# Scores and value products of a windowed attention kept together in TensorE's queue, with a new order of stages

## The chip, the cores and the metric

The kernel runs on one core of a Trainium2 chip. The metric is the device time of one execution, in microseconds (us). TensorE (PE in the profile, its weight loads PEld) multiplies matrices, VectorE (DVE), ScalarE (ACT) and GpSimd (POOL) do the work on elements, and SyncE (SP) issues nearly all transfers. Each engine takes its own queue strictly from the front.

## The reference

Eight sequences of 1024 tokens with 256 features, float32, pass through two blocks, each followed by a residual sum and a layer norm:

```
x = layernorm(x + attn(x))            # one causal head of width 64, biases, 8 x 1024 x 256
x = layernorm(x + ffn(x))             # ffn: two layers of:
    h   = shift_token(x)              # second half of the features comes from the token before
    q, k, v = split(h @ wqkv)         # 8 heads of 64
    q, k = l2norm(q)*qs, l2norm(k)*ks, then rotated and scaled by position
    o   = softmax over a window: a tile of 128 tokens sees itself and the tile before it
    x   = x + o @ wo
    h   = layernorm(shift_token(x)) * lg + lb
    a, g = split(h @ w1 + b1);  x = x + (a * gelu(g)) @ w2 + b2        # 682 hidden features
```

## The kernel before, in words

Matrix products of float32 precision are made of three products in a faster format: each operand is split into a high part (ScalarE, `halves`, L92) and a low part (VectorE, L93), and `products` (L104 does the matmuls) adds high x high, high x low and low x high in PSUM.

The program has two parts. `fronts` does the first attention and takes about the first 260 us; the change does not reorder it. `layers` does the two windowed layers. It walks over 128 tiles of 128 tokens (2 layers x 8 sequences x 8 tiles), two tiles in one pass of a loop, 64 pairs in all. A pass does not finish one pair: it runs a list of stages, `ORDER`, in which each entry names a stage and how far ahead of the current tile w it works. `("sc", -2, 0)` is the first half of the scores of tile w-2, `("qk", 1, 0)` the first half of the q and k of tile w+1. The stages:

- `prep` (L677): transposes two tiles of x (`l_xp`) into `l_xT`.
- `qk` (two halves, `l_pqk`): six matmuls of 512 columns; then ScalarE squares (L705), VectorE sums the squares (`l_ss`, L708) and multiplies twice by the rotary table (`l_t`, L715), GpSimd adds (L722).
- `v` (`l_pv`): six matmuls; ScalarE copies.
- `unit`: the inverse norms, a chain of ten small VectorE operations (`l_nrm_*`, L112 to L129), and two GpSimd products (L733).
- `turn` (two halves, `l_t`, L756): four transposes of q and k, split into `ring`.
- `sc` (two halves u, four heads each, `l_sc`, L785): twelve matmuls, whose operands have 64 rows. Heads go in pairs: one uses the upper, one the lower 64 rows of the array. Then, for each head, VectorE applies mask and scale in place and takes the extreme value (`l_nm`, L793), and ScalarE takes the exponential into `l_e` (L654). After the second half the inverse of the sums goes through DRAM and comes back spread over the partitions as `l_R` (L805 to L816).
- `et` (two halves, `l_et`, L832): eight transposes of e, copied by ScalarE into `l_eT` (L835).
- `val` (two halves, `l_po`, L849): eight matmuls of e and v, whose outputs have 64 partitions. Each is recorded as two passes.
- `out`: `l_po` times `l_R` on VectorE (`l_on`, L858), split on ScalarE (L863) and GpSimd (L864).
- `proj` (`l_py`): twelve matmuls, and VectorE adds x (L879).
- `side`: one step of the feed-forward of an earlier pair: norm and transposes (`m_hp`, L931), six steps of the first product (`m_pag`, L104; gelu on ScalarE, L966 and L969 on VectorE, L970 on GpSimd), two steps of the second product (`m_pf`, 17 matmuls each) and the end (L988). In the second layer the final norm (`o_*`) follows.

PSUM has eight banks. Four are the buffers of `l_sc` (`PSB["sc"]`); one half of a tile's scores takes two of them. The other four (`ps`) are shared by everything else that TensorE writes.

`ORDER` gives priorities, not the queues themselves. A planner that knows the data dependencies and models durations sets each engine's queue, and moves instructions of one stage between those of another where it expects an engine to be free. No order among matmuls is asked for beyond the data dependencies.

Of the kernel before, what the change touches and what calls it, by code (L numbers as in the profile page):

```python
# [28 lines left out]
def kernel(  # L29
# [31 lines left out]
    nc = tc.nc  # L61
# [33 lines left out]
    def products(dst, pairs):  # L95
# [4 lines left out]
        passes(dst, steps)  # L100

    def passes(dst, steps):
        for i, (a, b) in enumerate(steps):
            nc.tensor.matmul(dst, a, b, start=(i == 0), stop=(i == len(steps) - 1))  # L104

# [388 lines left out]
    def load_ffn(l, stage, ps, W):  # L494
# [22 lines left out]
        for c in range(2):  # L517
            pb = ps(f"pb1_{l}_{c}")
            for k in range(2):
                for m0, m1 in ((0, NF - 1), (NF - 1, NF + 1)):  # L520
# [4 lines left out]
                    for m in range(m0, m1):  # L525
                        z = P if m < NF else LEFT
                        q = 0 if m < NF else k * OFF
                        u = (m - m0) * P
                        nc.tensor.matmul(
                            pb[q : q + z, k * 8 + m : k * 8 + m + 1],  # L530
                            st[:, u : u + z], lgb[:, 1, c : c + 1], start=True, stop=True,
                        )
# [54 lines left out]
    ORDER = [  # L587
        ("side", 1), ("out", -4), ("side", 1), ("side", 1), ("unit", -1), ("proj", -4),
        ("unit", -2), ("turn", -2, 0), ("turn", -1, 0), ("turn", -1, 1), ("sc", -2, 0),
        ("turn", -2, 1), ("qk", 0, 0), ("out", -3), ("side", 1), ("sc", -2, 1), ("side", 1),  # L590
        ("side", 1), ("proj", -3), ("sc", -1, 0), ("qk", 0, 1), ("v", 1), ("et", -2, 0),
        ("sc", -1, 1), ("et", -2, 1), ("v", 0), ("et", -1, 0), ("val", -2, 0), ("et", -1, 1),
        ("prep", 2), ("qk", 1, 0), ("side", 1), ("side", 1), ("qk", 1, 1), ("val", -1, 0),
        ("val", -2, 1), ("val", -1, 1), ("side", 1), ("side", 1), ("side", 1),
    ]

    def layers(pool, psum):
# [59 lines left out]
        def attention(l, b, W, finished):  # L657
# [4 lines left out]
            def prep(p):  # L662
# [12 lines left out]
                for c in range(2):  # L675
                    for j in range(2):
                        nc.tensor.transpose(  # L677
                            pt[:, c, j * P : (j + 1) * P], xl[:, j, c * P : (c + 1) * P], ident
                        )
# [66 lines left out]
            def turn(t, k):  # L746
# [7 lines left out]
                for c in range(4):  # L754
                    cols = slice(c * P, (c + 1) * P)
                    nc.tensor.transpose(pt[:, cols], r[:, cols], ident)  # L756
                hi, lo = [x[:, :, 2 * k : 2 * k + 2, slot, :] for x in ring]
                halves(hi, lo, pt.rearrange("p (s c q) -> p s c q", s=2, c=2))

            def scores(w, u):  # L760
# [19 lines left out]
                for j in range(2):  # L780
                    c = 2 * u + j
                    for m, (x, y) in enumerate(((0, 0), (0, 1), (1, 0))):
                        for i in range(2):
                            rows = slice(i * DH, (i + 1) * DH)
                            nc.tensor.matmul(  # L785
                                sc[i][:, j, 0:nk], ring[x][rows, 0, c, slot, :],
                                ring[y][rows, 1, c, keys, :], start=(m == 0), stop=(m == 2),
                            )
                for j in range(2):
# [33 lines left out]
            def turn_e(w, u):  # L823
# [4 lines left out]
                for j in range(2):  # L828
                    pt = ps(f"{n}_et{j}").rearrange("p (a i q) -> p a i q", a=2, q=P)
                    for a in range(m):  # L830
                        for i in range(2):
                            nc.tensor.transpose(  # L832
                                pt[:, a, i, :], e[:, i, j, a * P : (a + 1) * P], ident
# [4 lines left out]
            def values(w, u):  # L838
# [5 lines left out]
                for j in range(2):  # L844
                    c = 2 * u + j
                    for a, t in enumerate(order):
                        for i in range(2):
                            head = 2 * c + i
                            nc.tensor.matmul(  # L849
                                po[i * DH : (i + 1) * DH, c * P : (c + 1) * P],  # L850
                                st["v", t][:, head * DH : (head + 1) * DH], eT[:, j, a, i, :],
                                start=(a == 0), stop=(a == len(order) - 1),
                            )

# [34 lines left out]
        def feed_forward(l, b, p, x1, W):  # L889
# [39 lines left out]
            for c in range(2):  # L929
                for j in range(2):  # L930
                    nc.tensor.transpose(  # L931
                        pt[:, c, j * P : (j + 1) * P], hn[:, j, c * P : (c + 1) * P], ident
# [100 lines left out]

        PAIRS = DEPTH * B * NT // 2

        run("prep", 0)
# [76 lines left out]
```

## Time and profile before

| | |
|---|---|
| median of 3 runs | 2795.12 us (2794.61 to 2795.77) |
| the profiled execution | 2790.89 us, span 2789.1 us, mean granted clock 0.984 |
| TensorE matmuls | busy 2703.2 us (97%), 22336 records |
| TensorE weight loads | busy 2350.4 us (84%) |
| VectorE | busy 2440.2 us (87%) |
| ScalarE | busy 1748.8 us (63%) |
| GpSimd | busy 1245.9 us (45%) |
| first transpose of `layers`, first one of the last pair | 261.5 us, 2661.9 us |

Busy is the time in which at least one instruction of the engine runs. Matmuls are pipelined: a matmul lasts 0.28 us in the records, but the next one starts 0.11 to 0.12 us after it. So the durations of matmuls don't add up to time, and the distance from one start to the next (the pitch) is what counts. "Idle before" is the time before an instruction in which its engine did nothing, with the releaser that ended it.

### The profile page before, as it was taken

To read this page: it belongs to the slowest core of one execution; us is meant where nothing else is said; L and a number is where in the kernel's file an instruction comes from. 1 tells how busy PE (TensorE), PEld (TensorE's weight loads), DVE (VectorE), ACT (ScalarE), POOL (GpSimd) and SP (SyncE) were. 2 spreads that over 40 slices of the span, in tenths; PEclk is the share of its full clock that TensorE was granted. 3 is DMA by queue.
4 is the path that set the end of the run, shared out by engine and by line. 5 is a ranking of instruction groups with operands and counts; after the bars stand their busy time and mean duration, and the time that the engine had idled before them with its cause. 6 is when DMAs were issued, how large, how long until landed. Compare 5 with 4: busy or idle time off the path is not lost.

```text
span 2789.1 us, 63147 instructions
## 1 busy us (share of the span) xinstructions
PE 2703.2 (97%) x22336; PEld 2350.4 (84%) x22336; DVE 2440.2 (87%) x8464; ACT 1748.8 (63%) x4486; POOL 1245.9 (45%) x1515
## 2 busy tenths in 40 slices
PE   7998999999999999999999999999999999999997
PEld 5776688888888888888888788888888888888886
DVE  6887789888889988889888899999999999999995
ACT  6675566666666666666666566666666666666663
POOL 4553244444444444344453444444444454444442
PEclk9999899999999999999999999999999999999998
DMA  6332011011111111111111111111111111111110
GB/s 181 97 98 86 26 39 43 28 43 43 43 41 39 34 38 43 43 41 39 37 57 52 57 51 49 39 41 49 51 50 40 39 48 50 51 41 43 43 47 24
DMA packets 146126, 139.83 MB, mean 50 GB/s; under 512 B 28680, under 2 KB 122768, under 8 KB 145808
## 3 DMA queue, kind: packets, MB, share of 16 engines
q1 hardware_dynamic: 144448, 135.32, 16.0%
q8 instruction: 176, 2.88, 0.4%
q14 instruction: 142, 1.16, 0.1%
q10 hardware_dynamic: 1360, 0.46, 0.1%
HBM read 95.35 MB, written 27.81 MB: 44 GB/s over the span
## 4 chain that ended last, share of the span: by engine, by line
PE 69%; DVE 22%; ACT 3%; DMA 3%; issue 2%; POOL 0%; SPq 0%; DVEq 0%; POOLq 0%; ACTq 0%
PE l_pqk L104 11%; PE m_pag L104 9%; PE m_pf L104 9%; PE l_sc L785 8%; PE l_et L832 7%; PE l_po L849 6%; PE l_pv L104 5%; PE l_py L104 4%; PE l_t L756 3%; DVE l_t L715 3%; DVE m_gl L966 3%; DVE m_a L969 2%; DVE l_nrm_p L127 1%; DVE l_ss L708 1%; DVE l_sc L793 1%
## 5 line engine op out<-in xcount | busy, mean ns | idle before, releaser
L722 POOL TENSOR_TENSOR l_t<-l_t,l_t 128x256 f32<-128x256 f32 x512 | 367.5, 739 | 855.1 <-DVE l_t L715 816.0
L654 ACT ACTIVATE l_e<-l_sc,l_nm 128x256 f32<-128x256 f32 (+1 forms) x992 | 450.6, 462 | 288.4 <-DVE l_nm L793 279.3
L104 PE MATMUL m_pag<-m_hT,w_h 128*128 128x256 f32 (+1 forms) x2816 | 515.1, 285 | 6.4 <-DVE l_t L715 3.3
L793 DVE CUSTOM_DVE_ANT_0 l_sc<-l_sc,mask,l_nrm_y 128x256 f32<-128x256 f32 (+1 forms) x1024 | 453.6, 470 | 50.6 <-ACT l_e L654 36.0
L104 PEld LDWEIGHTS m_pag<-m_hT,w_h 128*128 128x128 f32 (+1 forms) x2816 | 430.3, 187 | 21.1 <-issue 10.5
L654 ACT ACTIVATE m_gl<-m_pag,b 128x256 f32<-128x256 f32 (+1 forms) x384 | 181.4, 474 | 385.2 <-PE m_pag L104 332.6
L104 PE MATMUL m_pag<-m_hT,w_l 128*128 128x256 f32 (+1 forms) x1408 | 393.7, 280 | 0.0
L104 PE MATMUL l_pqk<-wqk_h,l_xT 128*128 128x512 f32 x1024 | 392.4, 424 | 0.8 <-ACT l_xT L92 0.8
L715 DVE TENSOR_TENSOR l_t<-l_pqk,l_tab 128x512 f32<-128x512 f32 x512 | 329.8, 680 | 0.0
L835 ACT COPY l_eT<-l_et 128x512 f32<-128x512 f32 (+1 forms) x512 | 276.0, 567 | 80.6 <-PE l_et L832 56.3
L970 POOL TENSOR_TENSOR m_a<-m_gl,m_a 128x256 fp32r<-128x256 f32 x320 | 241.4, 762 | 113.2 <-DVE l_nrm_h L125 55.4
L832 PE MATMUL l_et<-ident,l_e 128*128 128x128 f32 x1920 | 269.9, 279 | 4.4 <-ACT l_eT L835 3.4
L104 PEld LDWEIGHTS m_pag<-m_hT,w_l 128*128 128x128 f32 (+1 forms) x1408 | 264.7, 188 | 0.0
L832 PEld LDWEIGHTS l_et<-ident,l_e 128*128 128x128 f32 x1920 | 215.2, 141 | 49.9 <-ACT l_eT L835 13.3
L104 PE MATMUL m_pf<-w_h,m_a 128*128 128x256 f32 x1280 | 249.5, 284 | 0.0
L849 PE MATMUL l_po<-l_eT,l_v 128*64 128x128 f32 x3840 | 242.0, 278 | 0.7 <-ACT l_eT L835 0.6
L104 PEld LDWEIGHTS l_pqk<-wqk_h,l_xT 128*128 128x128 f32 x1024 | 196.0, 191 | 53.9 <-ACT l_xT L92 1.2
L849 PEld LDWEIGHTS l_po<-l_eT,l_v 128*64 128x64 f32 x3840 | 209.5, 138 | 35.2 <-issue 18.8
L104 PEld LDWEIGHTS m_pf<-w_h,m_a 128*128 128x128 f32 x1280 | 203.5, 188 | 11.0 <-POOL m_a L970 0.2
L864 POOL TENSOR_TENSOR l_oT<-l_on,l_oT 128x512 fp32r<-128x512 f32 x128 | 165.0, 1289 | 97.5 <-ACT l_oT L863 92.6
L785 PE MATMUL l_sc<-ring,ring 64*128 64x256 f32 (+1 forms) x2048 | 207.5, 283 | 0.0
L104 PE MATMUL l_py<-wo_h,l_oT 128*128 128x256 f32 x1024 | 205.0, 282 | 0.0
(195 smaller groups left out, 6636.4 us busy)
## 6 DMA issues: line engine op xcount, KB each, us to landing
l_R<-rd_d SPq DMA_DIRECT2D x256, 128.0 KB
x<-x_d SPq DMA_DIRECT2D x96, 256.0 KB
l_tab<-tab_d SPq DMA_DIRECT2D x128, 128.0 KB
xin<-in_L_attn_x_dram SPq DMA_DIRECT2D x16, 512.0 KB
x_d<-xin SPq DMA_DIRECT2D x16, 512.0 KB
rd_d<-l_rT SPq DMA_DIRECT2D x512, 1.0 KB
x_d<-x SPq DMA_DIRECT2D x32, 256.0 KB
out_dram<-x SPq DMA_DIRECT2D x32, 256.0 KB
```

The source lines that it names most:

```text
L104: nc.tensor.matmul(dst, a, b, start=(i == 0), stop=(i == len(steps) - 1))
L654: ins = nc.scalar.activation(*args, **kw)
L715: nc.vector.tensor_tensor(tt[j].rearrange("p (k h d) -> p k h d", k=2, d=DH), p3, tb.unsqueeze(2).to_broadcast([P, 2, HEADS // 2, DH]), AL ...
L722: nc.gpsimd.tensor_add(a[:, :, s, :], a[:, :, s, :], bsw[:, :, 1 - s, :])
L756: nc.tensor.transpose(pt[:, cols], r[:, cols], ident)
L785: nc.tensor.matmul(sc[i][:, j, 0:nk], ring[x][rows, 0, c, slot, :], ring[y][rows, 1, c, keys, :], start=(m == 0), stop=(m == 2),)
L793: nc.vector.tensor_tensor_reduce(dst, dst, mk, st["nrm", w][:, 8 * u + h : 8 * u + h + 1], BIG, ALU.add, ALU.min, nm[:, one],)
L832: nc.tensor.transpose(pt[:, a, i, :], e[:, i, j, a * P : (a + 1) * P], ident)
L835: nc.scalar.copy(eT[:, j, 0:m], pt[:, 0:m])
L849: nc.tensor.matmul(po[i * DH : (i + 1) * DH, c * P : (c + 1) * P], st["v", t][:, head * DH : (head + 1) * DH], eT[:, j, a, i, :], start=(a ...
L864: nc.gpsimd.tensor_tensor(oT[1], on, oT[0].bitcast(FP), ALU.subtract)
L970: nc.gpsimd.tensor_tensor(a[1], gl[0:z, :], a[0].bitcast(FP), ALU.subtract)
```

## The change

Two things change, both in `layers`; all arithmetic and all instructions that compute stay.

First, the matmuls and transposes of TensorE go through small wrappers, which add order edges from the start of `layers` on. An edge of this kind is no wait on a semaphore; it only tells the planner which of two TensorE instructions has to stand first in the queue. The matmuls of `sc` and `val` are marked `part=True`. Marked matmuls that are emitted one after the other are chained and form a group. The first one of a new group is put behind all unmarked ones that were emitted since the last group, and every unmarked one behind the last group. So nothing can be planned into a group, and nothing can move across one.

Second, `ORDER` is another permutation of the same 40 entries. In it the two halves of the scores of a tile stand next to each other, and so do the two halves of `val`, so that a group has the 24 score matmuls, or the 16 value matmuls, of all eight heads of 128 tokens.

```diff
+    group = {"on": False, "in": False, "free": [], "last": None}
+
+    def behind(ins, others):
+        for o in others:
+            tc.add_manual_dep(
+                ins, o.name,
+                mybir.DependencyInfo(
+                    mybir.DependencyClass.NoSync, mybir.DependencyReason.DATA
+                ),
+                reason="group",
+            )
+
+    def queued(ins, part):
+        g = group
+        if not g["on"]:
+            return
+        ins = ins.ins
+        if part and not g["in"] and g["free"]:
+            behind(ins, g["free"])
+        elif g["last"] is not None:
+            behind(ins, [g["last"]])
+        if part:
+            g["last"], g["free"] = ins, []
+        else:
+            g["free"].append(ins)
+        g["in"] = part
+
+    def matmul(*args, part=False, **kw):
+        queued(nc.tensor.matmul(*args, **kw), part)
+
+    def transpose(*args):
+        queued(nc.tensor.transpose(*args), False)
...
     ORDER = [
-        ("side", 1), ("out", -4), ("side", 1), ("side", 1), ("unit", -1), ("proj", -4),
-        ("unit", -2), ("turn", -2, 0), ("turn", -1, 0), ("turn", -1, 1), ("sc", -2, 0),
-        ("turn", -2, 1), ("qk", 0, 0), ("out", -3), ("side", 1), ("sc", -2, 1), ("side", 1),
-        ("side", 1), ("proj", -3), ("sc", -1, 0), ("qk", 0, 1), ("v", 1), ("et", -2, 0),
-        ("sc", -1, 1), ("et", -2, 1), ("v", 0), ("et", -1, 0), ("val", -2, 0), ("et", -1, 1),
-        ("prep", 2), ("qk", 1, 0), ("side", 1), ("side", 1), ("qk", 1, 1), ("val", -1, 0),
-        ("val", -2, 1), ("val", -1, 1), ("side", 1), ("side", 1), ("side", 1),
+        ("side", 1), ("side", 1), ("out", -4), ("side", 1), ("unit", -2), ("turn", -2, 0),
+        ("turn", -2, 1), ("unit", -1), ("out", -3), ("qk", 0, 0), ("qk", 0, 1), ("sc", -2, 0),
+        ("sc", -2, 1), ("turn", -1, 0), ("proj", -4), ("side", 1), ("turn", -1, 1), ("side", 1),
+        ("side", 1), ("proj", -3), ("et", -2, 1), ("sc", -1, 0), ("sc", -1, 1), ("et", -2, 0),
+        ("v", 1), ("v", 0), ("et", -1, 0), ("val", -2, 0), ("val", -2, 1), ("et", -1, 1),
+        ("side", 1), ("prep", 2), ("qk", 1, 0), ("side", 1), ("val", -1, 0), ("val", -1, 1),
+        ("qk", 1, 1), ("side", 1), ("side", 1), ("side", 1),
     ]
...
-                            nc.tensor.matmul(
+                            matmul(
                                 sc[i][:, j, 0:nk], ring[x][rows, 0, c, slot, :],
                                 ring[y][rows, 1, c, keys, :], start=(m == 0), stop=(m == 2),
+                                part=True,
                             )
...
-                            nc.tensor.matmul(
+                            matmul(
                                 po[i * DH : (i + 1) * DH, c * P : (c + 1) * P],
                                 st["v", t][:, head * DH : (head + 1) * DH], eT[:, j, a, i, :],
                                 start=(a == 0), stop=(a == len(order) - 1),
+                                part=True,
                             )
...
+        group["on"] = True
```

The queues of both programs can be laid side by side before either runs. On TensorE a pass of the steady state reads so (number of matmuls of the program in brackets; -2, -1, 0, 1 as in `ORDER`):

```
before  xp[4] pqk 1,0[6] hp[4] pqk 1,1[6] po -1[16] pag[66] py -4[12] t[16] sc -2,0[12]
        pqk 0,0[6] pf[17] sc -2,1[12] pf[17] py -3[12] sc -1,0[12] pqk 0,1[6] pv 1[6] et -2,0[8]
        sc -1,1[12] et -2,1[8] pv 0[6] et -1,0[8] po -2[16] et -1,1[8]
after   xp[4] pqk 1,0[6] hp[4] po -1[16] pqk 1,1[6] pag[66] t -2[8] pqk 0,0[6] pqk 0,1[6]
        sc -2[24] t -1,0[4] py -4[12] pf[17] t -1,1[4] pf[17] py -3[12] et -2,1[8] sc -1[24]
        et -2,0[8] pv 1[6] pv 0[6] et -1,0[8] po -2[16] et -1,1[8]
```

A stretch of neighbouring matmuls that use the array as 64 rows by 128 columns (`sc`), or as 128 rows by 64 columns (`po`), is called a visit here, since TensorE comes from matmuls of the full array and goes back to them. Over the whole program the visits of the 64-row kind go from 344 to 178 (50 of them in `fronts` in both), those of the 64-column kind from 192 to 187 (59 in `fronts`). That the numbers of the steady state are not all of them (4 x 64 = 256 visits by `sc` in the list, 294 in the queue) comes from places where the planner put single score matmuls between the transposes of `et`. Instructions on TensorE's queue that only wait for a semaphore go from 339 to 684.

More of the change, by code (lines that the diff above doesn't have):

```diff
@@ L100, in products @@
         passes(dst, steps)
+    group = {"on": False, "in": False, "free": [], "last": None}
[26 more added lines that the diff above has]
+        queued(nc.tensor.transpose(*args), False)
     def passes(dst, steps):
         for i, (a, b) in enumerate(steps):
-            nc.tensor.matmul(dst, a, b, start=(i == 0), stop=(i == len(steps) - 1))
+            matmul(dst, a, b, start=(i == 0), stop=(i == len(steps) - 1))
     def rsqrt(sm, src, n, low, op, name):
@@ L676, in prep @@
                     for j in range(2):
-                        nc.tensor.transpose(
+                        transpose(
                             pt[:, c, j * P : (j + 1) * P], xl[:, j, c * P : (c + 1) * P], ident
@@ L755, in turn @@
                     cols = slice(c * P, (c + 1) * P)
-                    nc.tensor.transpose(pt[:, cols], r[:, cols], ident)
+                    transpose(pt[:, cols], r[:, cols], ident)
                 hi, lo = [x[:, :, 2 * k : 2 * k + 2, slot, :] for x in ring]
@@ L831, in turn_e @@
                         for i in range(2):
-                            nc.tensor.transpose(
+                            transpose(
                                 pt[:, a, i, :], e[:, i, j, a * P : (a + 1) * P], ident
@@ L848, in values @@
                             head = 2 * c + i
-                            nc.tensor.matmul(
+                            matmul(
                                 po[i * DH : (i + 1) * DH, c * P : (c + 1) * P],
@@ L930, in feed_forward @@
                 for j in range(2):
-                    nc.tensor.transpose(
+                    transpose(
                         pt[:, c, j * P : (j + 1) * P], hn[:, j, c * P : (c + 1) * P], ident
```

## The prediction, made before the changed kernel was run

> **What bounds the kernel now.** I read the page's first part, then the busy time by stretches, then TensorE's timeline around one visit of the score matmuls.
>
> ```profile
> PE 2703.2 (97%) x22336; PEld 2350.4 (84%) x22336; DVE 2440.2 (87%) x8464; ACT 1748.8 (63%) x4486; POOL 1245.9 (45%) x1515
> ```
>
> 97% alone says little, since the ends of matmuls are modelled. The stretches say more; the first lies in layer 0, the second in layer 1 (columns: length, PE, PEld, DVE, ACT, POOL, granted clock, DMA share, GB/s):
>
> ```profile
> 500.00:1100.00 600.00, 599.44 (x5101) 531.60 (x5100) 533.53 (x1781) 387.74 (x989) 264.21 (x338) 1.00 0.13 40
> 1700.00:2600.00 900.00, 892.97 (x7540) 786.94 (x7539) 829.20 (x2959) 569.40 (x1436) 418.14 (x524) 1.00 0.15 46
> ```
>
> TensorE has no idle time in layer 0 and 0.8% in layer 1, at the full clock. VectorE is second: 89% and 92%. From the starts of `l_xp` on the timeline a pass of `ORDER` (two tiles) lasts 37.84 us in layer 0 and 38.57 us in layer 1. So VectorE works 0.889 x 37.84 = 33.6 us a pass in layer 0 and 0.921 x 38.57 = 35.5 us in layer 1; its gaps under 0.1 us add 0.6 us to each.
>
> The next view is TensorE's timeline from a `proj` over a half of scores to a `qk`. The first column is the start, the last the number of matmuls.
>
> ```profile
> 859.40 0.28 PE L104 MATMUL l_py<-wo_l,l_oT 128*128 128x256 f32 x1
> 859.52 0.28 PE L104 MATMUL l_py<-wo_h,l_oT 128*128 128x256 f32 x1
> 859.73 0.39 PE L785 MATMUL l_sc<-ring 64*128 64x256 f32 x2
> 859.95 0.40 PE L785 MATMUL l_sc<-ring,ring 64*128 64x256 f32 x4
> 860.19 0.28 PE L785 MATMUL l_sc<-ring 64*128 64x256 f32 x2
> 860.31 0.40 PE L785 MATMUL l_sc<-ring,ring 64*128 64x256 f32 x4
> 860.64 0.50 PE L104 MATMUL l_pqk<-wqk_h,l_xT 128*128 128x512 f32 x1
> 860.98 0.40 PE L104 MATMUL l_pqk<-wqk_l,l_xT 128*128 128x512 f32 x1
> ```
>
> Read the starts: `l_py` to `l_py` takes 0.12 us, `l_py` to the first `l_sc` 0.21, the first pair of heads to the second 0.22, a later pair 0.12, and the first `l_pqk` to the second 0.34. No wait is shown. Crossing between matmuls of the whole array and of 64 rows costs time, on the way in and out, and twice each time.
>
> **The change part by part.** *Visits removed.* The price of a crossing, from medians of the starts after 400 us. Into scores: first gap 0.203 to 0.217 instead of 0.109 to 0.122 (+0.092), second pair 0.220 instead of 0.115 (+0.105): 0.197 us. Out of scores into `qk` or `pf`: 0.207 instead of 0.117, then 0.340 instead of 0.233: 0.197 us. Out into transposes (`et`): +0.090, then 0.165 instead of 0.109: 0.146 us. Into `po`: 0.203 instead of 0.109, then 0.153 instead of 0.102: 0.145 us. Out of `po`: 0.204 us into `pag`, 0.156 us into `et`.
>
> In `layers` the queue before has 294 visits by scores, of which 100 leave into `et`: 294 x 0.197 + 194 x 0.197 + 100 x 0.146 = 110.7 us. After there are 128, all leaving into transposes: 128 x (0.197 + 0.146) = 43.9 us. Gain 66.8 us. For `po`, 133 visits (67 out into `et`) cost 43.3 us, and 128 (64 into `et`, 64 into `qk`, priced like `pag`) 41.7 us. Gain 1.6 us. **Together 68.4 us**, 1.07 us a pass. All of it is on TensorE's queue, which is the path. The sum stands against the profiled 2790.9 us (span 2789.1 and 1.8 around it), 4.2 us under the median; I carry the gain over to the median.
>
> [...]
>
> *What the edges add.* No instruction that computes. Instructions that only wait on TensorE's queue go from 339 to 684. Nearest row: about 115 of them stand before steps of `pag` today.
>
> ```profile
> L104 PE MATMUL m_pag<-m_hT,w_h 128*128 128x256 f32 (+1 forms) x2816 | 515.1, 285 | 6.4 <-DVE l_t L715 3.3 <-DVE l_xT L673 1.5 <-ACT m_hT L92 1.0
> ```
>
> All idle time there is 6.4 us, at most 0.056 us each, or 19 us for 345 more. But steps of `pag` start at 0.117 to 0.121 us like any other matmul, so I take 0.
>
> *Turns split up.* Today the sixteen transposes `t` stand together and take 2.14 us instead of 16 x 0.109 = 1.74, and the scores behind them 1.04 instead of 0.91: 0.53 us a pass waiting for VectorE and GpSimd. After, eight transposes follow `pag`, twelve `qk` matmuls (2.67 us) cover the split into `ring` before the scores, and the other transposes stand alone in front of `py` or `pf`. The stalls may vanish (34 us in 64 passes) or move.
>
> *The new wait.* 24 score matmuls need all four score banks at once, and behind them stands everything on TensorE. The first group finds banks free for 20 us. The second comes after t, py, pf, t, pf, py and `et -2,1`; that `et` itself needs the last exponential of the first group. Counted from the end of `pag`, TensorE reaches it at 0.88 (t) + 2.67 (qk) + 1.72 (24 scores) + 0.59 + 1.43 + 1.96 + 0.44 + 1.95 + 1.45 = 13.1 us. VectorE can start the sum of squares of the first `qk` at 0.88 + 1.28 + 0.6 = 2.8 us; its queue holds from there two `qk` (3.6 us at a pitch of 0.6), eight heads (3.2 us at 0.405), a `ring` (0.6), an `x` (0.45) and four steps of `unit` (0.8): 8.7 us, so 11.5, and the exponential 12.1. Slack: 1.0 us. Today `et -2,1` comes about 9 us after the scores of only four heads. VectorE's timeline today, where it bears on this:
>
> ```profile
> 842.12 0.73 DVE L119 SCALAR_TENSOR_TENSOR l_nrm_u<-l_nrm_t,l_nrm_i 128x16 f32<-128x16 f32 x1
> 842.88 0.18 DVE L121 SCALAR_TENSOR_TENSOR l_nrm_z<-l_nrm_u,l_nrm_i 128x16 f32<-128x16 f32 x1
> 849.27 0.31 DVE L969 CAST ax<-m_gl 42x256 fp32r<-42x256 f32 x1
> 853.71 0.49 DVE L793 CUSTOM_DVE_ANT_0 l_sc<-l_sc,mask,l_nrm_y 128x256 f32<-128x256 f32 x1 [0.23 <-ACT l_e L654]
> ```
>
> The first line holds a trap. GpSimd's instruction at the same time:
>
> ```profile
> 842.08 0.74 POOL L970 TENSOR_TENSOR m_a<-m_gl,m_a 128x256 fp32r<-128x256 f32 x1 [0.38 <-DVE l_nrm_t L117]
> ```
>
> The small step of `unit` ends when GpSimd's does: 0.73 instead of 0.16 to 0.18 us. In the new stretch GpSimd has four `l_t` of 0.72 us and an `l_oT` of 1.29 us, 4.2 of about 7 us. Four steps that are caught 6 times in 10 cost 4 x 0.6 x 0.57 = 1.4 us: 0.4 us more than the slack.
>
> Is VectorE on time at all? Today it ends the last step of `pag` (`ax`) at 849.6, 2.9 us behind the matmuls (846.6), since two chains of `unit` and an `on` lie in that stretch. After, one chain and no `on` lie there, 2.8 + 0.6 us less. And its heads alternate over four banks, so the wait of 0.23 us for the exponential in the same bank goes (36.0 us in the list of waits). In layer 1 nine steps of `o_rs` at 0.2 us and four others of about 0.3 come between the two groups, 3 us a pass, and `et -1,0`, 3.7 us behind the second group, just about covers them: 0.4 to 1.0 us there. So new stalls of 0.4 us a pass in layer 0 and 0.7 in layer 1, 0.55 in the mean. Of the old ones I credit the 0.40 in the transposes and not the 0.13 in the scores. Net 0.15 us a pass, 64 x 0.15 = 9.6 us.
>
> *Moved transfers.* On SP's queue the two table loads stand together, before the copies `m_sh` and the trip of the sums through DRAM. The table buffers come free half a pass earlier, and `l_R` is used over 5 us after its request, so 0. If `m_sh` lands 1 us late, VectorE waits under the cover of `pv` (2.67 us); without that cover it is 64 us.
>
> **Forecast:** 2795.1 - 68.4 + 9.6 = 2736.3 us. Its own range: 2705 (68.4 and 22 of the 34 us of today's stalls) to 2762 (0.55 us a pass of new stalls, 35 us, and nothing credited); the 19 us of waiting instructions would make 2755, inside it.
>
> **The rivals.** *VectorE caps layer 1.* It needs 35.5 + 0.6 = 36.1 us of a pass, and TensorE would want 37.5. Work bunched around the groups could keep layer 1 at 38.57; then only layer 0 gains, 32 x 1.07 = 34 us: 2761, and 2780 if half of that goes too. For it: 92% busy. Against: 1.4 us of room. [...]
>
> *The second group waits: slower.* If all four steps of `unit` are caught (2.3 us) and VectorE is behind as today, which makes it 1.3 us late at the first sum of squares, the stall at `et -2,1` is 2.3 + 1.3 - 1.0 = 2.6 us a pass: 2795 + 64 x (2.6 - 1.07) = 2893 us. With the steps alone 1.3 us, so 2810, which I take as its price. It decides from 1.07 us a pass. For it: 24 score matmuls need what the exponentials of eight heads set free, while TensorE can do nothing else. Against: VectorE is 3.4 us lighter ahead of it.
>
> *The crossing is not what costs.* If the gaps belong to first loads after a wait, fewer visits leave them, and the time stays at 2795. Against: `py` to `t` and `pag` to `py` change operands too, and start 0.119 and 0.116 us apart.
>
> **How the numbers follow.** Forecast 0.72 (0.04 of it below 2705), VectorE's cap 0.15, group waits 0.10, crossing costs nothing 0.03. The range 2705 to 2780 holds 0.68 and 0.13, about 8 in 10. About 0.2% (5.6 us) can be told from no change: faster 0.87, same 0.03, slower 0.10.
>
> **What would show it.** The 64-row visits: 24 matmuls in one run, late only in the first two pairs and behind the last; passes of about 36.8 to 37.2 us in layer 0 and 37.3 to 37.9 in layer 1; VectorE at 91% and 94%. Right or wrong on the slack: idle time of TensorE in front of `l_et` with releaser ScalarE `l_e`, or in front of `l_sc`; a pass of over 37.8 us in layer 0 would refute the forecast. If the gaps at the crossings stay as many in time as before, the third rival holds.

## The result, and the profile after

The change makes the kernel **slower: 2866.7 us** (median of 4 runs, 2865.2 to 2869.9) against 2795.4 us, a ratio of 1.0257 (95% interval 1.0239 to 1.0275). Forecast were 2736.3 us and a range of 2705 to 2780. The profiled execution has a span of 2863.4 us, 74.3 us more than before.

The first part of the page of after, to be laid beside the same line of before:

```profile
PE 2655.7 (93%) x22336; PEld 2346.7 (82%) x22336; DVE 2431.9 (85%) x8464; ACT 1742.3 (61%) x4486; POOL 1254.0 (44%) x1515
```

All busy times but GpSimd's have fallen, and the span has grown: the loss is idle time. The busy time by stretches, the first in layer 0 and the second in layer 1 (start and end, length, PE, PEld, DVE, ACT, POOL, clock, DMA share, GB/s) says where:

```profile
500.00:1100.00 600.00, 590.41 (x5166) 534.36 (x5164) 529.68 (x1798) 390.34 (x995) 270.10 (x344) 1.00 0.14 40
1700.00:2600.00 900.00, 812.93 (x6852) 721.95 (x6851) 763.43 (x2707) 519.70 (x1322) 379.31 (x470) 0.97 0.14 42
```

Layer 0 does more matmuls in 600 us than before (5166 against 5101). Layer 1 does 6852 in 900 us instead of 7540, TensorE is idle for 87 us of them, and the granted clock is 0.97. From one first `l_xp` of a pass to the next, a pass lasts 37.32 us in layer 0 (before 37.84) and 42.40 us in layer 1 (before 38.57; 28 and 24 passes). In the trace the difference of 74 us is made of 0.9 us up to the first pass, -19.9 us in the first 31 passes, -1.8 us in the seven between the layers, +92.1 us in 24 passes of layer 1, and +3.1 us behind them.

The chain that ended last names a line that before has not ("DMA x<-x_d 3%"), and the list of waits puts it first (total, times, longest, in us; L132 and L135 are the lines of the wrappers `matmul` and `transpose`):

```profile
PE l_xp L135 <- DMA x<-x_d: 88.9, 29, 4.7
PE l_et L135 <- ACT l_e L689: 19.3, 31, 2.0
PE l_pqk L132 <- DVE m_gl L1003: 12.4, 59, 0.2
```

There are 29 waits, about one for each pass of layer 1: the transposes of `prep` wait for x to be loaded. Two timelines of after show one of them, SP's issues first, then TensorE:

```profile
2179.01 0.41 SPq L661 DMA_DIRECT2D out_dram<-x  x1
2180.07 1.48 SPq L846 DMA_DIRECT2D rd_d<-l_rT  x4
2182.03 0.39 SPq L656 DMA_DIRECT2D x<-x_d  x1
2182.67 1.15 SPq L852 DMA_DIRECT2D l_R<-rd_d  x2
```
```profile
2180.09 0.66 PE L135 MATMUL l_et<-ident,l_e 128*128 128x128 f32 x4 [0.20 <-ACT l_eT L871]
2184.98 1.09 PE L135 MATMUL l_xp<-ident,x 128*128 128x128 f32 x4 [4.23 <-DMA x<-x_d]
2185.71 0.77 PE L132 MATMUL l_pqk<-wqk_h,l_xT 128*128 128x512 f32 x1
2186.29 0.63 PE L132 MATMUL l_pqk<-wqk_l,l_xT 128*128 128x512 f32 x1
```

TensorE is through with `et` at 2180.75 and has nothing ahead of `l_xp` to do. The load of its x is issued only at 2182.03, behind the store of a finished output (2179.01), and lands at about 2184.9. Read also the starts behind it: `l_pqk` to `l_pqk` takes 0.58 us instead of 0.33. The granted clock by stretches, of the 5 us before the wait and the 5 us behind it:

```profile
2176.00:2181.00 5.00, 3.98 (x35) 2.79 (x33) 4.86 (x29) 5.00 (x18) 0.00 (x0) 1.00 0.19 57
2185.00:2190.00 5.00, 5.00 (x20) 3.98 (x22) 1.59 (x5) 1.67 (x3) 0.67 (x1) 0.50 0.24 75
```

Behind this wait the granted clock stays at 0.50 until about 2190.8; from 2191 to 2192 it is 1.00. Against the run without the wait (`prepfirst`, below), the stretch from the last `et` to the first `xp` has 3.2 us a pass more, and the rest of the pass 0.45 us more: 0.44 in the `qk` just behind and 0.21 in `po`, less 0.21 us that prepfirst waits between `xp` and `qk`.

The matmuls that were joined do what the prediction says of them. TensorE's timeline of after, a group of 24 scores between `qk` and `t`:

```profile
802.97 0.40 PE L132 MATMUL l_pqk<-wqk_h,l_xT 128*128 128x512 f32 x1
803.30 0.39 PE L132 MATMUL l_sc<-ring 64*128 64x256 f32 x2
803.52 0.40 PE L132 MATMUL l_sc<-ring,ring 64*128 64x256 f32 x4
...
804.48 0.28 PE L132 MATMUL l_sc<-ring 64*128 64x256 f32 x2
804.60 0.40 PE L132 MATMUL l_sc<-ring,ring 64*128 64x256 f32 x4
804.93 0.66 PE L135 MATMUL l_t<-ident,l_t 128*128 128x128 f32 x4
```

The first score starts 0.33 us behind a `qk` matmul of 512 columns (two such matmuls start 0.23 to 0.24 us apart), the second pair of heads 0.22 us behind the first, all others 0.12 us apart.

### The profile page after: what moved, and what is told of

Read it like the earlier page. It is cut to its first block, busy times and chain, and to the rows that moved or that the text cites. A ratio compares the mean times of both kernels' runs of the same rounds, so it can differ in the third digit from the quotient of the medians.

```text
span 2863.4 us, 63425 instructions
## 1 busy us (share of the span) xinstructions
PE 2655.7 (93%) x22336; PEld 2346.7 (82%) x22336; DVE 2431.9 (85%) x8464; ACT 1742.3 (61%) x4486; POOL 1254.0 (44%) x1515
## 4 chain that ended last, share of the span: by engine, by line
PE 47%; DVE 33%; ACT 10%; DMA 6%; issue 2%; SPq 1%; POOL 0%; DVEq 0%; POOLq 0%; ACTq 0%
PE l_pqk L132 13%; PE l_po L132 7%; ACT l_e L689 5%; PE m_pf L132 5%; PE l_sc L132 5%; DVE m_gl L1003 4%; PE l_et L135 4%; DVE l_t L750 4%; PE l_py L132 3%; DVE l_sc L829 3%; DMA x<-x_d 3%; DVE m_a L1006 2%; PE l_pv L132 2%; DVE l_ss L743 2%; DVE l_nrm_p L162 2%
## 5 line engine op out<-in xcount | busy, mean ns | idle before, releaser
L757 POOL TENSOR_TENSOR l_t<-l_t,l_t 128x256 f32<-128x256 f32 x512 | 374.3, 753 | 508.1 <-DVE l_t L750 339.0
L132 PE MATMUL m_pag<-m_hT,w_h 128*128 128x256 f32 (+1 forms) x2816 | 506.9, 282 | 3.1 <-DVE l_t L750 2.0
L829 DVE CUSTOM_DVE_ANT_0 l_sc<-l_sc,mask,l_nrm_y 128x256 f32<-128x256 f32 (+1 forms) x1024 | 443.3, 466 | 21.4 <-PE l_sc L132 11.3
L132 PEld LDWEIGHTS m_pag<-m_hT,w_h 128*128 128x128 f32 (+1 forms) x2816 | 436.2, 188 | 9.9 <-ACT m_gl L689 2.4
L132 PE MATMUL l_pqk<-wqk_h,l_xT 128*128 128x512 f32 x1024 | 384.4, 426 | 17.8 <-DVE m_gl L1003 12.4
L132 PE MATMUL m_pag<-m_hT,w_l 128*128 128x256 f32 (+1 forms) x1408 | 395.6, 281 | 0.0
L740 ACT ACTIVATE l_sq<-l_pqk 128x512 f32<-128x512 f32 x256 | 153.2, 599 | 352.0 <-PE l_pqk L132 350.7
L135 PE MATMUL l_et<-ident,l_e 128*128 128x128 f32 x1920 | 276.8, 280 | 41.1 <-ACT l_e L689 19.3
L135 PEld LDWEIGHTS l_et<-ident,l_e 128*128 128x128 f32 x1920 | 212.5, 142 | 90.9 <-ACT l_eT L871 31.0
L1007 POOL TENSOR_TENSOR m_a<-m_gl,m_a 128x256 fp32r<-128x256 f32 x320 | 248.3, 791 | 65.3 <-DVE l_nrm_h L160 50.1
L958 POOL TENSOR_TENSOR x<-x,b 128x512 f32<-128x512 f32 x64 | 84.2, 1316 | 439.6 <-DVE m_hn L954 292.2
L132 PEld LDWEIGHTS l_pqk<-wqk_h,l_xT 128*128 128x128 f32 x1024 | 200.1, 195 | 85.6 <-DVE m_gl L1003 26.7
L132 PEld LDWEIGHTS m_pag<-m_hT,w_l 128*128 128x128 f32 (+1 forms) x1408 | 266.1, 189 | 0.0
L768 POOL TENSOR_TENSOR l_t<-l_t,l_nrm_y 128x256 f32<-128x256 f32 x256 | 155.0, 626 | 249.5 <-DVE l_nrm_y L164 241.4
L132 PE MATMUL m_pf<-w_h,m_a 128*128 128x256 f32 x1280 | 249.6, 283 | 0.0
L132 PE MATMUL l_po<-l_eT,l_v 128*64 128x128 f32 x3840 | 243.7, 280 | 0.0
L743 DVE TENSOR_REDUCE l_ss<-l_sq 128x8 f32<-128x512 f32 x256 | 174.8, 683 | 69.0 <-ACT l_sq L740 67.6
```

The lines of the kernel that those rows point to most:

```text
L132: queued(nc.tensor.matmul(*args, **kw), part)
L135: queued(nc.tensor.transpose(*args), False)
L740: nc.scalar.activation(sq, pqk, AF.Square)
L743: nc.vector.tensor_reduce(st["ss", t][:, k * HEADS : (k + 1) * HEADS], sq.rearrange("p (g d) -> p g d", d=DH), AX.X, ALU.add)
L757: nc.gpsimd.tensor_add(a[:, :, s, :], a[:, :, s, :], bsw[:, :, 1 - s, :])
L768: nc.gpsimd.tensor_tensor(kk, kk, n4[:, k, 1, :].unsqueeze(2).to_broadcast([P, HEADS // 2, DH]), ALU.mult,)
```

## The experiments

Where the new `ORDER` puts `prep` matters through a line that the diff does not show. `prep`'s tile of x and a second load of x in `feed_forward` (x0, for the residual, in layer 1 alone) take their buffers from one pool of five, and buffers are handed out in program order. Before, `("prep", 2)` stood ahead of the first `side` of a new feed-forward, which asks for x0. In the new `ORDER` a `("side", 1)` stands in front of it. SP's queues, from the programs (layer 1; `x_1_3_2`: layer, sequence, pair):

```
before  out  x0_2_3  rd_d[4]  l_R[2]  x_1_3_3 ...  out  x0_3_0  rd_d[4]  l_R[2]  x_1_4_0
after   out  rd_d[4]  x_1_3_2  l_R[2]  x0_3_0 ...  out  rd_d[4]  x_1_3_3  l_R[2]  x0_3_1
```

At the same place of the pass, before loads the x of `prep` one pair further ahead. After loads x0 a pass early instead, and `prep`'s x takes the buffer that the store has just set free. That is theory A: the loss is this wait. The rival B says that grouping makes VectorE and the banks late, and the wait for x only shows it.

The first four runs are set against runs of before with a median of 2793.1 us.

**prepfirst**: the change, with two entries exchanged.

```diff
-        ("side", 1), ("prep", 2), ("qk", 1, 0), ("side", 1), ("val", -1, 0), ("val", -1, 1),
+        ("prep", 2), ("side", 1), ("qk", 1, 0), ("side", 1), ("val", -1, 0), ("val", -1, 1),
```

> The changed kernel with two neighbouring entries of ORDER exchanged: ("prep", 2) in front of the first ("side", 1) behind proj -3, as in the old ORDER. Theory A (buffers): the five x buffers are handed out in the order in which they are asked for; in the changed kernel the feed-forward asks for its copy of x0 before prep asks for the next pair, so in layer 1 prep's load waits for the store of an earlier pair's output and TensorE waits for the load. With the exchange prep's load goes out one pass earlier: layer 1 falls from 42.4 to 37.3 to 38.3 us a pass, the wait of l_xp for x goes, layer 0 stays at 37.3; 32 x 4.1 to 5.1 us less than 2866.7, so 2703 to 2736. Theory B (VectorE or the second group of scores is what is late in layer 1): a load that comes earlier moves the stall to l_et or l_sc, layer 1 stays over 41 us a pass, time over 2820.

Measured: 2763.8 us (2761.1 to 2768.0), ratio 0.9891 (0.9875 to 0.9908). Layer 1 falls from 42.40 to 38.76 us a pass, and of the waits for x only the one of the first pass is left, which before has too:

```profile
PE l_xp L135 <- DMA x<-x_d: 4.7, 1, 4.7
```

So 102.9 of the 130 us between forecast and result are the wait for x. Theory B (over 2820) is refuted, but the time misses theory A's 2703 to 2736 as well: the rest has another cause, 27.5 us above the forecast.

**x6**: the change, with a sixth buffer for x (and one `sq` less, for space).

```diff
-            "sq": 6, "t": 6, "v": 4, "eT": 2, "oT": 2, "on": 1, "R": 2, "xT": 4, "hT": 2, "hn": 1,
-            "sh": 3, "a": 10, "gl": 3, "x": 5, "tab": 2,
+            "sq": 5, "t": 6, "v": 4, "eT": 2, "oT": 2, "on": 1, "R": 2, "xT": 4, "hT": 2, "hn": 1,
+            "sh": 3, "a": 10, "gl": 3, "x": 6, "tab": 2,
```

> The changed kernel with six x buffers instead of five (and five instead of six of the squares' buffers, for space), ORDER as in the change. Theory A: the sixth buffer does the same as the exchange of prep and side: layer 1 at 37.3 to 38.3 us a pass, 2703 to 2736 us; by the buffers alone, no stage is moved. Theory B: no more than 20 us gained. A third theory, that SP's queue (the issues of the sums' trip in front of the load) delays the load and not the buffer, expects that the load still goes out behind the same issues and 2 us before it is needed: 2840 or more.

Measured: 2762.2 us, ratio 0.9892 (0.9876 to 0.9908). It leaves `ORDER` alone and gives as much as prepfirst, 104.5 us: it is the buffer, and not the place of `prep` on TensorE's queue. The third theory of the expectation, a load that SP's issues hold up (2840 or more), falls with it. The time again lies above 2703 to 2736.

**joined**: the edges and the old order, in which only halves are pulled together (`turn -2`, `sc -2`, `sc -1`, `et -2`, `val -2`).

```diff
-        ("unit", -2), ("turn", -2, 0), ("turn", -1, 0), ("turn", -1, 1), ("sc", -2, 0),
-        ("turn", -2, 1), ("qk", 0, 0), ("out", -3), ("side", 1), ("sc", -2, 1), ("side", 1),
-        ("side", 1), ("proj", -3), ("sc", -1, 0), ("qk", 0, 1), ("v", 1), ("et", -2, 0),
-        ("sc", -1, 1), ("et", -2, 1), ("v", 0), ("et", -1, 0), ("val", -2, 0), ("et", -1, 1),
+        ("unit", -2), ("turn", -2, 0), ("turn", -2, 1), ("turn", -1, 0), ("turn", -1, 1),
+        ("sc", -2, 0), ("sc", -2, 1), ("qk", 0, 0), ("out", -3), ("side", 1), ("side", 1),
+        ("side", 1), ("proj", -3), ("qk", 0, 1), ("sc", -1, 0), ("sc", -1, 1), ("v", 1),
+        ("et", -2, 0), ("et", -2, 1), ("v", 0), ("et", -1, 0), ("val", -2, 0), ("val", -2, 1),
+        ("et", -1, 1),
...
```

> The edges with the old ORDER, in which only the halves are joined: sc -2,0 with sc -2,1 behind the turns, sc -1,0 with sc -1,1 behind qk 0,1, val -2,1 with val -2,0; sides, prep, unit, out and proj stay where they were. Visits by scores 128 in layers, by values 128, as in the change. Theory A: prep stands in front of the sides, so no wait for x; the gain of the crossings (1.07 us a pass) less what the joined groups wait for. Sixteen transposes stand in front of the first group as before (0.5 us stall), and ring is needed right behind them (another 0.5 to 1.5 us). 2720 to 2790. Theory B: layer 1 over 41 us a pass here too, 2830 or more.

Measured: 2811.6 us, ratio 1.0068 (1.0053 to 1.0083), between the two expectations. It has 128 visits by scores as well, but its passes of layer 0 last 38.64 us (before 37.84). In this order sixteen `et` stand behind a single `pv`, and they wait for a bank of `ps` that ScalarE's copy of v sets free (over the whole program):

```profile
PE l_et L135 <- ACT l_v L778: 29.2, 42, 1.2
PE l_pv L132 <- ACT l_eT L871: 16.6, 54, 1.5
```

ScalarE's timeline shows why the copy is late: in one pass of layer 0 it starts at 838.44, behind three exponentials of the joined group (837.08 to 838.4) that VectorE released late, and `et` goes on at 839.08. So joining in this order, without new cover for the waits, loses more than the crossings give.

**noedge**: the new order without the edges: 320 visits by scores in `layers`, not 128.

```diff
-        group["on"] = True
```

> The changed kernel's new ORDER without the order edges. The planner puts score matmuls between transposes again: 320 visits by scores in layers instead of 128, the load of x as in the change. If a visit costs the 0.34 us of the prediction where transposes are its neighbours: 192 more, 66 us, of which layer 0's half shows at once (38.3 instead of 37.3 us a pass), while in layer 1 a part may vanish in the wait for x: 2890 to 2935. If crossings cost nothing: 2860 to 2875. Theory A: layer 1 keeps its wait of l_xp for x of 2 to 3 us a pass.

Measured: 2922.3 us, inside 2890 to 2935 and 55.6 us more than with the edges, ratio 1.0462 (1.0445 to 1.0479). The waits for x are there too (61.1 us from 1500 to 2500 us; 65.7 there in after): they come from the order, not from the edges.

The next four are set against runs of before with a median of 2793.5 us.

**valfirst**: prepfirst, with the values ahead of the transposes that wait in layer 1.

```diff
-        ("v", 1), ("v", 0), ("et", -1, 0), ("val", -2, 0), ("val", -2, 1), ("et", -1, 1),
+        ("v", 1), ("v", 0), ("val", -2, 0), ("val", -2, 1), ("et", -1, 0), ("et", -1, 1),
```

> The order with prep ahead of the side step, and besides val -2,0 and val -2,1 moved ahead of et -1,0, so that 32 po matmuls (1.9 us) lie between the v matmuls and the transposes that wait in layer 1. No crossing is added (128 visits by scores, 128 by po). Theory 'one uncovered wait': what is left of layer 1's loss stands in front of et -1,0 (2.29 us for the v-to-et stretch instead of 1.00), since ScalarE's exponentials of the second group end late there; covered, the pass of layer 1 falls from 38.8 to 37.5-37.9 us and the time from 2764 to 2728-2742. Rival 'VectorE caps layer 1': the wait comes back at the next place, the pass stays at 38.4-38.8 and the time at 2753-2766.

Measured: 2786.5 us, ratio 0.9975 (0.9963 to 0.9987): 23 us slower than prepfirst. Both expectations miss. The old wait for `l_e` is gone from the list, but 16 transposes stand together now, and TensorE waits inside them for banks of `ps` that `l_on` and the copy of v still hold (waits of valfirst, 500 to 1100 us):

```profile
PE l_et L135 <- DVE l_on L895: 8.3, 16, 1.3
PE l_et L135 <- ACT l_v L778: 3.5, 4, 1.6
```

The stretch from the last `po` to the last `et` takes 2.88 us in layer 0, 1.0 us more than 16 transposes at 0.11 us behind a crossing.

**prepfirst_noedge**: prepfirst without edges: again 320 visits by scores, and no wait for x.

```diff
-        group["on"] = True
+        group["on"] = False
```

> The order with prep ahead of the side step, without the order edges: 320 visits by scores in the layers instead of 128, 137 by po instead of 128, and no wait for x. Theory 'crossings cost what the gaps show' (0.197 in, 0.146 to 0.197 out): 192 x 0.36 + 3 = 72 us at most over the kernel with edges, less what the scheduler's freer queue hides of other waits: 2764 + 50 to 72 = 2814-2836. Rival 'the edges only shift the waits': within 20 us of it, 2755-2784.

Measured: 2810.9 us, ratio 1.0066 (1.0048 to 1.0084), 47.1 us above prepfirst: below the expected 2814 to 2836, and far from the rival's 2755 to 2784. In layer 0 a pass lasts 38.11 instead of 37.29 us with five visits instead of two. About 0.20 us of waits are gone with it, in front of `et -1,1` (1.18 us from the last `po` to the last `et` instead of 1.35) and between the last `xp` and the sixth `qk` matmul (1.33 instead of 1.36), so three visits cost 0.82 + 0.20 = 1.02 us, 0.34 us each. The prices taken give 0.34 to 0.39. Crossings cost what the gaps show, and a part of what is saved is waited for elsewhere: in layer 1 the three visits cost only 0.67 us a pass net (39.43 instead of 38.76).

**b_lateprep**: the kernel before, with one `side` put ahead of `prep`, no edges.

```diff
-        ("prep", 2), ("qk", 1, 0), ("side", 1), ("side", 1), ("qk", 1, 1), ("val", -1, 0),
+        ("side", 1), ("prep", 2), ("qk", 1, 0), ("side", 1), ("qk", 1, 1), ("val", -1, 0),
```

> The kernel before with one change: a side step put ahead of prep 2 in its old order, so that feed_forward takes its x buffer first; no edges, no other move. Theory 'the x buffers are handed out in program order, and prep's load then waits for the store of an output': layer 1 waits at l_xp for the load of x, 3 to 4.5 us a pass, and the time is 2880-2940. Rival 'the wait for x comes from the grouping of matmuls': no wait at l_xp, 2785-2810.

Measured: 2843.6 us, ratio 1.0180 (1.0164 to 1.0195). The sign and the place are those of the buffer theory, the size is half (2880 to 2940 were expected): a pass of layer 1 lasts 40.33 us, layer 0 keeps its 37.84, and the waits of layer 1 are these (1500 to 2500 us; there is none of this kind there in before):

```profile
PE l_xp L677 <- DMA x<-x_d: 24.0, 12, 3.3
PE l_xp L677 <- ACT l_eT L835: 12.6, 10, 1.5
```

In this queue the load stands directly behind the store, ahead of the four `rd_d`, and so it comes earlier than in after. One entry of `ORDER`, with no grouping at all, makes the wait.

**b_x6**: the kernel before with the buffers of x6.

> The kernel before with 6 buffers x and 5 buffers sq, as the run x6 had them on the kernel after. If x6 gained by ending the wait for x, this gains nothing, since before has no such wait: 2785-2802. If it is the buffers as such that help: 30 us or more faster, under 2770. If the fifth buffer sq costs something, it shows here: over 2805.

Measured: 2796.6 us, ratio 1.0010 (0.9997 to 1.0024). The buffers as such change nothing; x6 gained only what it took away from the wait.

The last runs ask what is left in prepfirst (runs of before: 2791.9 us, for outlast 2790.0). Its list of waits begins:

```profile
PE l_et L135 <- ACT l_e L689: 19.3, 31, 2.0
PE l_pqk L132 <- DVE m_gl L1003: 13.6, 60, 0.9
```

The second comes in nearly every pass of both layers (60 times in 64). TensorE and VectorE in after (prepfirst has the same):

```profile
799.08 1.03 PE L135 MATMUL l_t<-ident,l_t 128*128 128x128 f32 x8
800.32 0.50 PE L132 MATMUL l_pqk<-wqk_h,l_xT 128*128 128x512 f32 x1 [0.21 <-DVE m_gl L1003]
```
```profile
798.88 0.48 DVE L1003 SCALAR_TENSOR_TENSOR m_gl<-m_pag,b,m_gl 128x256 f32<-128x256 f32 x1
799.40 0.48 DVE L1006 CAST m_a<-m_gl 128x256 fp32r<-128x256 f32 x1
799.79 0.47 DVE L1003 SCALAR_TENSOR_TENSOR m_gl<-m_pag,b,m_gl 128x256 f32<-128x256 f32 x1
```

Behind `pag` two `t` and then `qk` want banks of `ps`, one every 0.44 us. The bank for `qk` is the one of the fifth `pag`; its gelu product on VectorE runs from 799.79 to 800.26, behind a cast that TensorE does not wait for here, and `qk` starts at 800.32. The recorded idle time is 0.21 us, but from the last `t` to `qk` it is 0.48 instead of 0.03 (castlate, below): this wait is more than its entry in the list, since matmul ends are modelled.

**castlate**: prepfirst, with that cast behind that product.

```diff
...
-                nc.vector.tensor_copy(a[0], gl[0:z, :])
-                nc.gpsimd.tensor_tensor(a[1], gl[0:z, :], a[0].bitcast(FP), ALU.subtract)
+                if m == NF - 1:
+                    behind(split(*held), [prod.ins])      # cast of step m-1 behind the product of step m
+                if m == NF - 2:
+                    held = a, gl
+                else:
+                    split(a, gl[0:z, :])
...
```

`split` issues the two removed lines, `prod` is the gelu product.

> The order with prep ahead of the side step, and one VectorE step moved: the cast of the fourth gelu product stands behind the fifth product, whose bank of ps the first qk matmul waits for. TensorE's queue is unchanged. Theory 'qk 0,0 waits for a bank of ps that the gelu product sets free': the stretch from t to qk falls from 3.13 to 2.7-2.85 us in both layers, 0.3 to 0.4 us a pass, and the time from 2764 to 2738-2746. Rival 'the next bank or the split into ring is late then': the gap moves to the next stretch, 2757-2768.

Measured: **2735.8 us** (2733.5 to 2739.4), ratio 0.9803 (0.9788 to 0.9819), 28 us under prepfirst and a little under the expected 2738 to 2746. From the last `t` through the twelve `qk` matmuls it takes 2.68 us instead of 3.14 in layer 0 and 2.67 instead of 3.15 in layer 1; a pass lasts 36.91 and 38.24 us. A single VectorE step, put behind its neighbour, is worth 1% of the kernel. It is the fastest version found.

In prepfirst and castlate the first wait of the list stands in layer 1 alone: from the last `pv` to the last `et -1,0` it is 2.27 us there and 1.00 in layer 0. VectorE's timeline of prepfirst has the reason. The first pair of heads of the second group is computed from 2123.00 to about 2123.7 (six matmuls, the last starting at about 2123.34), but VectorE comes to it at 2125.15:

```profile
2122.38 0.68 DVE L1025 TENSOR_TENSOR x<-m_pf,x 128x512 f32<-128x512 f32 x1
2123.10 0.75 DVE L172 BATCH_NORM_STATS2 o_st<-x 128x6 f32<-128x256 f32 x2
...
2124.68 0.15 DVE L147 TENSOR_SCALAR o_rs_a<-o_mv 128x2 f32<-128x2 f32 x1
2124.87 0.17 DVE L149 TENSOR_SCALAR o_rs_i<-o_rs_a 128x2 int32<-128x2 int32 x1
2125.07 0.16 DVE L152 TENSOR_TENSOR o_rs_t<-o_rs_a,o_rs_i 128x2 f32<-128x2 f32 x1
2125.15 0.48 DVE L829 CUSTOM_DVE_ANT_0 l_sc<-l_sc,mask,l_nrm_y 128x256 f32<-128x256 f32 x1
```

The norm of the output, which layer 0 has not, stands ahead of the softmax steps.

**outlate**: prepfirst, with feed_forward's last step behind the second group (`last` runs it), and `o_st` by an order edge behind the group's softmax steps.

```diff
-        ("side", 1), ("proj", -3), ("et", -2, 1), ("sc", -1, 0), ("sc", -1, 1), ("et", -2, 0),
+        ("proj", -3), ("et", -2, 1), ("sc", -1, 0), ("sc", -1, 1), ("last", 1), ("et", -2, 0),
...
-            nc.vector.bn_stats(stats[:, j, :], part)
+            s = nc.vector.bn_stats(stats[:, j, :], part)
+            if late and tail["sc"] is not None:
+                behind(s.ins, [tail["sc"]])
...
```

> The order with prep ahead of the side step, and the last step of feed_forward (in layer 1 the normalisation of the output, o_st and o_rs) moved behind the second group's scores, on VectorE behind its softmax steps by an order edge. TensorE's queue is unchanged. Theory 'the normalisation stands ahead of the second group's softmax steps on VectorE and makes the exponentials late that et -1,0 needs': the stretch from v to et in layer 1 falls from 2.29 to 1.0-1.3 us, layer 0 keeps its 37.3 us, and the time is 2725-2742. Rival 'VectorE caps layer 1': the delay comes back at hp or pqk behind xp, layer 1 stays at 38.4 or more: 2752-2768.

Measured: 2863.6 us, ratio 1.0256 (1.0239 to 1.0272), 100 us slower than prepfirst and outside both expectations. The cause was named rightly, `pv` to `et` falls to 1.00 us. But the price is paid elsewhere: `m_rs`, on which `m_hn` and so the transposes `hp` depend, now alternates with `o_rs`. From the sixth `qk` matmul to the last `hp` it is 4.37 us instead of 0.69:

```profile
PE m_hp L135 <- DVE m_hn L958: 99.2, 59, 7.3
```

**both_x6**: outlate and castlate together, with the buffers of x6 (the three diffs above).

> The two VectorE moves together, with 6 buffers x and 5 sq besides. If the two waits are separate, their gains add: 2764 - 20 to 26 - 22 to 38 = 2700-2722, which is near the 2736 forecast for the change, since it removes what that forecast had not counted. If both are VectorE's load in another place, 2745-2765.

Measured: 2850.9 us, ratio 1.0229 (1.0209 to 1.0249). Layer 0 has 36.80 us a pass, layer 1 42.07: outlate's fault, which a sixth buffer does not mend. Both expectations (2700 to 2722, 2745 to 2765) miss.

**outlast**: castlate with the buffers of x6, and the norm of the output in a stage of its own, behind `m_hn` by an order edge.

```diff
-        ("prep", 2), ("side", 1), ("qk", 1, 0), ("side", 1), ("val", -1, 0), ("val", -1, 1),
+        ("prep", 2), ("side", 1), ("qk", 1, 0), ("side", 1), ("last", 1), ("val", -1, 0), ("val", -1, 1),
...
-                    nc.vector.tensor_scalar(
+                    tail["ins"] = nc.vector.tensor_scalar(
                         hn[:, i, c * P : (c + 1) * P], src, mv[:, i, 0:1], r[:, i : i + 1],
...
+            s = nc.vector.bn_stats(stats[:, j, :], part)
+            if late and tail["ins"] is not None:
+                behind(s.ins, [tail["ins"]])
...
```

> As castlate, with the normalisation of the output (o_st, o_rs, in layer 1) taken out of feed_forward's last step and put behind m_hn of the next feed_forward, on VectorE by an order edge, so that neither the second group's softmax steps nor m_hn wait for it; 6 buffers x and 5 sq, so that the later store holds up no load. TensorE's queue is unchanged. Theory 'what is left of the loss in layer 1 is work of VectorE in the wrong place': the stretch v to et falls from 2.29 to 1.0 us, hp stays on time, layer 1 goes from 38.24 to 36.9-37.5 us, and the time from 2736 to 2695-2715. Rival 'VectorE caps layer 1' (95% busy at 37.2 us): the 4 us of o_st and o_rs make l_on, l_xT or the sums of squares late instead, layer 1 stays at 38.0 or more, 2728-2745.

Measured: 2753.4 us, ratio 0.9871 (0.9848 to 0.9893), 18 us slower than castlate and above both ranges. `et` and `hp` are on time (1.00 and 0.56 us), and now other stages wait: from `qk` to the end of `pag` it is 9.08 us instead of 7.91, from the first `t` to `qk` 1.30 instead of 0.81, and from the last `xp` to the sixth `qk` matmul 1.80 instead of 1.58. Layer 1 takes 38.98 us a pass, castlate 38.24. By stretches, in outlast:

```profile
1700.00:2550.00 850.00, 818.86 (x7048) 727.12 (x7047) 798.29 (x2774) 533.76 (x1359) 391.94 (x485) 1.00 0.15 45
```

VectorE is 94% busy there (92% in castlate's layer 1). In three places the same steps of the norm, about 4 us a pass, make different stages late. That speaks for the rival "VectorE caps layer 1". It is not proved that no order would do: only these three were run.

## Why the prediction was wrong

**The step that failed is "Moved transfers ... so 0".** It followed the table loads, `l_R` and `m_sh` past each other on SP's queue, and left out the two loads of x. `prep` and the first `side` of a feed-forward change places in the new `ORDER`; both ask for a buffer x, in program order, and the later one gets the one that is set free last. The queues laid side by side had it: the x of the next pair was loaded one pair ahead in one and not in the other. In the runs that step is +103 us (after less prepfirst), more than the 68.4 us of all gains together. Who asks for a buffer before whom was not among the things it looked at.

**The second step is a missing one: the shared banks of `ps`.** The four banks of the scores were followed closely, the other four not at all. `qk 0,0` stands earlier behind `pag` in the new order, and wants a bank that VectorE hasn't emptied: 0.47 us a pass in both layers, 28 us by castlate. Another 0.33 us a pass of layer 0 stands in front of `et -1,1` (1.36 us from the last `po` through `et` instead of 1.03; the list of waits names the copy of v, 6 times and up to 1.8 us each in 900 us of layer 0).

**What was right.** The crossings cost what was taken. In layer 0, where 4 visits by scores a pass become 2, their prices give 2 x 0.197 on the way in, and 3 x 0.197 + 0.146 less 2 x 0.146 on the way out, together 0.84 us; the stalls among the transposes (0.43 us) and in the scores behind them (0.19) went, as foreseen; the new waits are 0.47, 0.33 and 0.09 us (`xp` to `qk`). That is -0.57 us a pass; measured are -0.52 (37.32 us, just above the foreseen 36.8 to 37.2). The slack at `et -2,1` held: it starts 0.119 us behind `py`, and its eight transposes are at pitch. The waiting instructions that the edges add cost nothing that shows; the group of `pag` has less idle time than before (6.4 us):

```profile
L132 PE MATMUL m_pag<-m_hT,w_h 128*128 128x256 f32 (+1 forms) x2816 | 506.9, 282 | 3.1 <-DVE l_t L750 2.0
```

**Layer 1 after that.** Foreseen were 0.7 us of new stalls and a pass of 37.3 to 37.9 us. There are 1.3 us at `et -1,0` alone, for which the prediction had 0.4 to 1.0 us, and 38.24 us in castlate, which no longer waits for the bank. Here the rival "VectorE caps layer 1" is nearer. That prepfirst's 2763.8 lies by the rival's 2761 is chance, though: 0.52 us of its 38.76 us a pass in layer 1 go with the bank of `ps` in castlate (38.24), layer 0 gained 0.55 us a pass and not the rival's 1.07, and VectorE is 92% busy and not full. A part of the waits that were left is for steps that read PSUM: `m_gl` (13.6 us in front of `l_pqk` in prepfirst's list), `l_on` (2.5 us there) and the copy of v (10.1 us in front of `l_et`). But what made the product late (castlate) was a cast that reads no PSUM, and what made the softmax steps late was the norm of x, which reads none either.

**The rivals.** "The second group waits" gave the right sign, 2810 to 2893 us, by a wait that is not there: `et -2,1` starts on time. joined has a relative of it, where layer 0 loses 0.80 us a pass: the exponentials of a joined group make `et` late, but by way of the copy of v behind them and its bank of `ps`. The list names `l_v` there, and not the `l_e` that the rival needs. "The crossing is not what costs" is refuted by noedge and prepfirst_noedge: 55.6 and 47.1 us for 192 more visits.

That castlate's 2735.8 us lie on the forecast of 2736.3 is partly chance: layer 0 has the foreseen pass (36.8 to 37.2, measured 36.91), layer 1 does not, and the seven passes between the layers gained 15 us (280.8 instead of 295.5) where 7 x 1.07 = 7.5 us was counted.

## What to carry to other kernels

When stages are permuted, follow each pool of buffers as well as each engine: list who asks for a buffer, in program order, and see which request now comes behind which release; a load that moves behind a store can cost more than the whole permutation gains (here 103 us against the 68.4 us counted). Two programs' DMA queues laid side by side show it before a run. For a wait that is left, look at what stands one instruction ahead of the releaser on its engine: here one cast in front of one product cost 28 us, while moving larger work on an engine that is 92% busy only moved the wait (outlate was 100 us slower than prepfirst, outlast 18 us slower than castlate).

## What the runs showed of the hardware

In after the waits of TensorE for x cost more than their length. Behind the one of 4.23 us shown above the granted clock was 0.50 up to about 2190.8, and 512-column matmuls started 0.42 to 0.58 us apart instead of 0.23 to 0.33; in layer 1 the rest of a pass was 0.45 us longer, net, than in prepfirst, on top of 3.2 us of waiting. Some shorter ones were followed by it too. Of the 28 waits of `l_xp` for x in after, from the second one on, all nine of 3.28 us or more were followed by half clock, and seven of the nineteen of 2.47 to 2.92 us (the six `qk` matmuls behind them start over 1.43 us or more instead of 1.23 to 1.26): after one of 2.56 us at 2609.4 the clock was 0.50 from 2610.8 to 2614.0, after one of 2.54 us at 2399.7 it was 1.00 from 2401.0 to 2404.4. So a wait of 2.56 us was followed by half the clock here, and one of 2.92 us, at 1762.5, was not: between these the length alone did not decide.

In outlate a VectorE step of two elements a row, on the path to `m_hn`, ended only when GpSimd's instruction beside it did:

```profile
2134.53 1.24 DVE L160 TENSOR_TENSOR m_rs_h<-m_rs_t,m_rs_z 128x2 f32<-128x2 f32 x1
```
```profile
2134.32 1.44 POOL L905 TENSOR_TENSOR l_oT<-l_on,l_oT 128x512 fp32r<-128x512 f32 x1 [9.11 <-ACT l_oT L904]
```

It took 1.24 us, where `o_rs_h`, the same step of the other norm, took 0.16 at 2132.64; both lines above end at about 2135.77. What held it is not shown.
